# A Restormer block on one core: an order written by a list scheduler, the tensor-engine convolution in 5 of 8 bands, two taps added by DMA, LayerNorm statistics in batches

## The chip, the core and the metric

One Trainium2 chip; the kernel runs on one of its cores, and the others are idle. The metric is device time in microseconds (us). Engines are named as in the profile: PE (TensorE, matmuls), DVE (VectorE), ACT (ScalarE), POOL (GpSimd) and SP (SyncE, which here only issues DMAs).

## The reference

One transformer block on 16 images of 128 channels and 96 x 96 pixels, all in float32. Cut to what matters:

```python
xn1 = layernorm(x_hwc, ln1_w, ln1_b)                 # over the 128 channels of each pixel
q, k, v = xn1 @ wq.T, xn1 @ wk.T, xn1 @ wv.T         # 8 heads of 16 channels
attn = softmax(einsum('bhcn,bhdn->bhcd', l2norm(q), l2norm(k)) * 16 ** -0.5)   # 16 x 16 per head
x = x + (einsum('bhcd,bhdn->bhcn', attn, v) merged over heads) @ wp.T
xn2 = layernorm(x_hwc, ln2_w, ln2_b)
h1 = einsum('bchw,oc->bohw', xn2, w_in)              # 128 -> 512 channels
h2 = depthwise 3 x 3 convolution of h1, padding 1    # 512 channels
x = x + einsum('bchw,oc->bohw', gelu(h2), w_out)     # 512 -> 128 channels
```

The attention is over channels, so for one image it is a 128 x 128 matrix that is applied to every pixel.

## The kernel before

An image is cut into 24 **units** of 4 rows (384 pixels, three tiles of 128) and 8 **bands** of 12 rows (three units). Channels lie on the partitions. An image goes through these steps:

- **LN1** (`ln1_unit`, with `normalised`), once per unit: PE transposes three 128 x 128 tiles to PSUM (L175), DVE takes their statistics (`bn_stats` L179, `bn_aggr` L180) and adds eps (`ve`, L182), POOL raises the variances to the power -0.5 (`rstd`, L184), DVE makes the shift (`nb`, L186), ACT applies scale and shift (L189), PE transposes back (L195) and adds the tile's products to the Gram matrix (L206), and ACT copies the normalised pixels into one of two padded image buffers `xn` (L210).
- **The matrix** (`attention`): some 30 small dependent operations make one 128 x 128 matrix for the image from its Gram matrix.
- **LN2** (`ln2_unit`), once per unit: PE multiplies the matrix with the unit (L298), DVE adds result and x (L300), and then the LayerNorm steps follow as above, with L302 at the end.
- **FFN**, once per band and each of four chunks of 128 hidden channels. Three chunks go `by_taps`: PE makes the hidden rows (L311, three matmuls), ACT copies them to SBUF (L314) and makes the first tap into the accumulator tile `h3` (L315), DVE adds the other eight taps one by one to `h3` in place (L318), and ACT applies Gelu (L321). This is called a **job** below. The fourth chunk goes `by_matmuls`: `w_in` and the convolution as one 3 x 3 convolution, nine matmuls a unit into PSUM (L330), with Gelu on ACT (L334).
- **Output** (`ffn_out`), once per unit: four matmuls (L340), DVE adds x (L345), and a band is stored by a DMA from SP.

The order of the work is that of the loops at the end: while the FFN of image i runs band by band, the list `beside` holds LN1 of image i + 1, the matrix, and LN2 two bands ahead, and its entries are dealt out between the steps of the band. The framework's own scheduler may move instructions a little within an engine's queue. Each engine executes its queue in order. x is loaded once and stays in SBUF from LN1 until the band is stored (`xpool`, 13 bands).

Of the kernel before, what the change touches and what calls it, by code (L numbers as in the profile page):

```python
# [22 lines left out]
def tile_restormer_block(  # L23
# [134 lines left out]
    h1p = ctx.enter_context(tc.tile_pool(name="h1p", bufs=2))  # L158
    h3p = ctx.enter_context(tc.tile_pool(name="h3p", bufs=2 * NCH))
# [7 lines left out]
    def x_unit(i, u):  # L167
        b, s = divmod(u, UPB)
        return xbs[i, b][:, s * UT : (s + 1) * UT]

    def normalised(xt, name):
        """z of a unit, with the pixels on the partitions (SBUF) and back on the free axis (PSUM)."""
        pT = p_tr.tile([P, TPU, P], F32, tag="tr", name=f"pT_{name}")
        for j in range(TPU):
            nc.tensor.transpose(pT[:, j, :], xt[:, j * P : (j + 1) * P], ident)  # L175
        st = small.tile([P, TPU, 6], F32, tag="st", name=f"st_{name}")
        mv = small.tile([P, TPU, 2], F32, tag="mv", name=f"mv_{name}")
        for j in range(TPU):
            nc.vector.bn_stats(st[:, j, :], pT[:, j, :])  # L179
            nc.vector.bn_aggr(mv[:, j, :], st[:, j, :])  # L180
        ve = small.tile([P, TPU], F32, tag="ve", name=f"ve_{name}")
        nc.vector.tensor_scalar(ve, mv[:, :, 1], EPS, None, ALU.add)  # L182
        rstd = small.tile([P, TPU], F32, tag="rstd", name=f"rstd_{name}")
        nc.gpsimd.tensor_tensor(rstd, ve, mhalf[:, :TPU], ALU.pow)  # L184
        nb = small.tile([P, TPU], F32, tag="nb", name=f"nb_{name}")
        nc.vector.scalar_tensor_tensor(nb, mv[:, :, 0], -1.0, rstd, ALU.mult, ALU.mult)  # L186
        zT = xhp.tile([P, TPU, P], F32, tag="zT", name=f"zT_{name}")
        for j in range(TPU):
            nc.scalar.activation(  # L189
                zT[:, j, :], pT[:, j, :], AF.Identity,  # L190
                bias=nb[:, j : j + 1], scale=rstd[:, j : j + 1],
            )
        pB = p_tr.tile([P, UT], F32, tag="tr", name=f"pB_{name}")
        for j in range(TPU):
            nc.tensor.transpose(pB[:, j * P : (j + 1) * P], zT[:, j, :], ident)  # L195
        return zT, pB

    grams, sums, mats = {}, {}, {}

    def ln1_unit(i, u):  # L200
        if u == 0:
            grams[i] = p_g.tile([P, P], F32, tag="g", name=f"g_{i}")
            sums[i] = keep.tile([P, NU], F32, tag="sums", name=f"sums_{i}")
        zT, pB = normalised(x_unit(i, u), f"a{i}_{u}")
        for j in range(TPU):
            nc.tensor.matmul(  # L206
                grams[i], lhsT=zT[:, j, :], rhs=zT[:, j, :],
# [221 lines left out]
```

## Time and profile before

| | |
|---|---|
| timed runs | 6691.94, 6692.86, 6698.94 us; median 6692.86 |
| profiled execution | its time is its span, 6694.6 us from the first to the last instruction |
| PE busy | 5776.3 us, 86% |
| DVE busy | 5447.8 us, 81% |
| ACT busy | 3065.7 us, 46% |
| POOL busy | 1158.9 us, 17% |
| DMA traffic | 155.62 MB, mean 23 GB/s |

Busy time is the union of an engine's instructions, DMA issues left out. A matmul's end is modelled, and successive matmuls overlap, so PE's busy time holds more than the array's work. A float32 matmul appears as two rows (x3456 matmuls of the composite convolution as x6912). In the chain of work each piece begins where the one before it released it, so the pieces of one engine in a row are the steps from one start to the next, shorter than the instruction's own record.

### The profile page before, as it was taken

The page shows a single profiled execution, that of the slowest core. Times are in us where ns is not written, and L with a number is a line of the kernel's source. Part 1 is how long each engine was busy: PE and PEld are TensorE (multiplying, and loading weights), DVE is VectorE, ACT ScalarE, POOL GpSimd, SP SyncE. Part 2 cuts the span into 40 slices and gives each one's busy share as a digit, 9 for nine tenths or more (in the row PEclk, how much of TensorE's full clock was granted, in tenths as well). Part 3 has the DMA queues.
Part 4 walks back from the last instruction along what each step waited for, and adds up shares of the span by engine and source line. Part 5 has one row for each costly group of instructions (what it writes and reads, how often), then busy time and mean ns, then how long its engine had stood idle before and what let it go on. Part 6 is the DMA issues. An engine that isn't in the chain of part 4 may idle for free.

```text
span 6694.6 us, 59531 instructions
## 1 busy us (share of the span) xinstructions
PE 5776.3 (86%) x20421; PEld 3234.1 (48%) x20421; DVE 5447.8 (81%) x10303; ACT 3065.7 (46%) x5808; POOL 1158.9 (17%) x802
## 2 busy tenths in 40 slices
PE   4888889888888888888888898888988889888899
PEld 3444445444454454544444454444544445444454
DVE  2778878888888888888888888887888888888899
ACT  2444444444444444444444444444444444444443
POOL 1111211212112111111212112121121211211100
PEclk6899999999999999999999999999999999999999
DMA  1000000000000000000000000000000000000000
GB/s 51 15 22 15 29 22 22 22 29 22 22 26 25 22 22 22 29 22 22 25 25 22 29 22 22 22 22 29 22 22 22 29 22 22 22 29 22 11 15 22
DMA packets 39520, 155.62 MB, mean 23 GB/s; under 512 B 5296, under 2 KB 6320, under 8 KB 39216
## 3 DMA queue, kind: packets, MB, share of 16 engines
q1 hardware_dynamic: 36864, 151.01, 6.6%
q8 instruction: 160, 2.62, 0.2%
q14 instruction: 144, 1.18, 0.1%
q10 hardware_dynamic: 2352, 0.81, 0.0%
HBM read 76.30 MB, written 75.50 MB: 23 GB/s over the span
## 4 chain that ended last, share of the span: by engine, by line
DVE 52%; PE 23%; POOL 16%; ACT 4%; issue 4%; POOLq 0%; DMA 0%; ACTq 0%
DVE h L318 37%; POOL rstd_a L184 10%; PE pc L330 7%; POOL rstd_b L184 6%; PE ph L311 4%; DVE st_a L179 3%; DVE st_b L179 3%; PE pB_b L195 3%; DVE xb L300 2%; PE g L206 2%; PE po L340 2%; PE pT_b L175 2%; ACT zT_b L189 1%; DVE mv_a L180 1%; PE pB_a L195 1%
## 5 line engine op out<-in xcount | busy, mean ns | idle before, releaser
L318 DVE SCALAR_TENSOR_TENSOR h<-h,dw,h 128x1152 f32<-128x1152 f32 x3072 | 4293.9, 1407 | 15.5 <-ACT h L315 7.9
L330 PE MATMUL pc<-xn,comp 128*128 128x384 f32 x6912 | 2386.4, 491 | 0.0
L330 PEld LDWEIGHTS pc<-xn,comp 128*128 128x128 f32 x6912 | 1281.4, 192 | 881.1 <-ACT h L314 80.8
L340 PE MATMUL po<-h,woutT 128*128 128x384 f32 x3072 | 1154.2, 502 | 187.9 <-ACT h L321 109.0
L184 POOL TENSOR_TENSOR rstd_a<-ve_a,mhalf 128x3 f32<-128x3 f32 x384 | 688.7, 1793 | 2835.2 <-DVE ve_a L182 2441.1
L311 PE MATMUL ph<-xn,winT 128*128 128x490 f32 (+1 forms) x2304 | 1040.3, 569 | 47.3 <-ACT h L314 40.7
L189 ACT ACTIVATE zT_a<-pT_a,nb_a,rstd_a 128x128 f32<-128x128 f32 x1152 | 443.4, 454 | 988.8 <-DVE nb_a L186 988.8
L340 PEld LDWEIGHTS po<-h,woutT 128*128 128x128 f32 x3072 | 555.3, 192 | 648.0 <-ACT h L321 171.8
L184 POOL TENSOR_TENSOR rstd_b<-ve_b,mhalf 128x3 f32<-128x3 f32 x384 | 439.8, 1145 | 2390.0 <-DVE ve_b L182 2086.4
L314 ACT COPY h<-ph 128x490 f32<-128x490 f32 (+1 forms) x1152 | 610.8, 541 | 386.1 <-PE ph L311 383.9
L321 ACT ACTIVATE h<-h 128x1152 f32<-128x1152 f32 x384 | 446.8, 1164 | 677.3 <-DVE h L318 677.3
L195 PE MATMUL pB_a<-ident,zT_a 128*128 128x128 f32 x1152 | 357.6, 314 | 344.8 <-ACT zT_a L189 343.9
L189 ACT ACTIVATE zT_b<-pT_b,nb_b,rstd_b 128x128 f32<-128x128 f32 x1152 | 442.8, 453 | 449.8 <-DVE nb_b L186 449.6
L311 PEld LDWEIGHTS ph<-xn,winT 128*128 128x128 f32 x2304 | 391.5, 194 | 482.8 <-ACT h L314 149.3
L179 DVE BATCH_NORM_STATS2 st_b<-pT_b 128x6 f32<-128x128 f32 x1152 | 296.9, 280 | 328.0 <-PE pT_b L175 327.5
L334 ACT ACTIVATE h<-pc 128x384 f32<-128x384 f32 x384 | 188.4, 491 | 807.9 <-PE pc L330 807.9
L315 ACT ACTIVATE h<-h,dw 128x1152 f32<-128x1152 f32 x384 | 483.2, 1258 | 9.1
L195 PE MATMUL pB_b<-ident,zT_b 128*128 128x128 f32 x1152 | 354.5, 316 | 131.3 <-ACT zT_b L189 118.2
L206 PE MATMUL g<-zT_a 128*128 128x128 f32 x2304 | 447.5, 293 | 0.0
L195 PEld LDWEIGHTS pB_a<-ident,zT_a 128*128 128x128 f32 x1152 | 170.7, 148 | 569.3 <-ACT zT_a L189 565.0
L206 PEld LDWEIGHTS g<-zT_a 128*128 128x128 f32 x2304 | 402.5, 219 | 3.1 <-issue 3.1
L195 PEld LDWEIGHTS pB_b<-ident,zT_b 128*128 128x128 f32 x1152 | 162.0, 141 | 458.0 <-ACT zT_b L189 402.4
(101 smaller groups left out, 3506.5 us busy)
## 6 DMA issues: line engine op xcount, KB each, us to landing
xb<-in_x_dram SPq DMA_DIRECT2D x128, 576.0 KB, 3.8
out_dram<-xb SPq DMA_DIRECT2D x128, 576.0 KB, 2.8
win_sb<-in_L_conv_w_in_dram ACTq DMA_DIRECT2D x1, 256.0 KB, 10.9
wout_sb<-in_L_conv_w_out_dram ACTq DMA_DIRECT2D x1, 256.0 KB, 12.5
wv_sb<-in_L_conv_wv_dram ACTq DMA_DIRECT2D x1, 64.0 KB, 4.7
wqk_sb<-in_L_conv_wq_dram ACTq DMA_DIRECT2D x1, 64.0 KB, 2.5
wqk_sb<-in_L_conv_wk_dram ACTq DMA_DIRECT2D x1, 64.0 KB, 2.4
wp_sb<-in_L_conv_wp_dram ACTq DMA_DIRECT2D x1, 64.0 KB, 4.1
```

The lines of the kernel that those rows point to most:

```text
L179: nc.vector.bn_stats(st[:, j, :], pT[:, j, :])
L184: nc.gpsimd.tensor_tensor(rstd, ve, mhalf[:, :TPU], ALU.pow)
L189: nc.scalar.activation(zT[:, j, :], pT[:, j, :], AF.Identity, bias=nb[:, j : j + 1], scale=rstd[:, j : j + 1],)
L195: nc.tensor.transpose(pB[:, j * P : (j + 1) * P], zT[:, j, :], ident)
L206: nc.tensor.matmul(grams[i], lhsT=zT[:, j, :], rhs=zT[:, j, :], start=(u == 0 and j == 0), stop=(u == NU - 1 and j == TPU - 1),)
L311: nc.tensor.matmul(ph, lhsT=winT[:, n, :], rhs=xn[:, r0 + r : r0 + r + k, :], start=True, stop=True)
L314: nc.scalar.copy(h1[:, r : r + k, :], ph)
L315: nc.scalar.activation(h3, h1[:, 0:BR, 0:W], AF.Copy, scale=dw[:, n, 0:1])
L318: nc.vector.scalar_tensor_tensor(h3, h1[:, dy : dy + BR, dx : dx + W], dw[:, n, t : t + 1], h3, ALU.mult, ALU.add)
L321: nc.scalar.activation(h3, h3, AF.Gelu)
L330: nc.tensor.matmul(pc, lhsT=comp[:, t, :], rhs=xn[:, r : r + UR, dx : dx + W], start=(t == 0), stop=(t == 8),)
L340: nc.tensor.matmul(rows(po), lhsT=woutT[:, n, :], rhs=hs[n][:, s * UR : (s + 1) * UR, :], start=(k == 0), stop=(k == NCH - 1),)
```

## The change

The loops at the end are replaced by a planner in the source. Every operation is entered in a list with its engine, a supposed duration, a place (a number that says how urgent it is), and what it reads and writes; `Plan.order` then plays engines and buffers through with these supposed durations, takes on each free engine the ready operation with the lowest place, and the operations are emitted in the order of their supposed starts, under `tc.manual_schedule()`, so that the framework moves none. The supposed time until an adding DMA has landed is `T_ADD`, 6500 ns. With it:

- The composite convolution on PE is used only in bands 1, 3, 5, 6 and 7; in bands 0, 2 and 4 the fourth chunk goes by taps too. Its nine matmuls a unit are nine entries of the list.
- Of a job's taps, ACT makes taps 1 and 2 as products in tiles `pr`; POOL issues a DMA that adds the second product to the first, and, after DVE's six other taps, one that adds the sum to `h3`. Gelu follows that DMA.
- LayerNorm works on batches of two units: the six tiles' `bn_stats` are combined by five DVE operations instead of `bn_aggr` and `ve`, and power and `nb` are made once per batch.
- x is loaded twice: for LN1 into a pool of two bands, and again for LN2 into one of six bands.
- PSUM: transposes back have a buffer of their own, outputs one instead of two, and the matrix step works in the Gram matrix's bank.

```diff
-UR = 4  # image rows of a unit: 384 tokens, three tiles of 128
...
+PE_BANDS = (1, 3, 5, 6, 7)
+DMA_TAPS = (1, 2)
+BU = 2
+ATT = 3.0
+LEAD = 3.0
+X1_BUFS, XB_BUFS, H1_BUFS, PR_BUFS, H3_BUFS = 2, 6, 3, 3, 9
+IN_TURN = ("h3", "h1", "pr", "xb", "x1")
+IN_ORDER = ("PE", "DVE", "ACT")
+SLACK = 300
+T_ADD = 6500
...
+        def dispatch(engine, time):
+            queue = queues[engine]
+            while queue:
+                item = heapq.heappop(queue)
+                k = item[1]
+                lacks = room(k)
+                if lacks is None:
+                    break
+                waiting.setdefault(lacks, []).append(k)
+            else:
+                return
...
+        return [ops[k][3] for k in sorted(range(len(ops)), key=lambda k: (starts[k], k))]
...
-    xpool = ctx.enter_context(tc.tile_pool(name="xpool", bufs=NB + 5))
+    xpool = ctx.enter_context(tc.tile_pool(name="xpool", bufs=XB_BUFS))
+    x1pool = ctx.enter_context(tc.tile_pool(name="x1pool", bufs=X1_BUFS))
     p_tr = ctx.enter_context(tc.tile_pool(name="p_tr", bufs=3, space=PSUM))
+    p_b = ctx.enter_context(tc.tile_pool(name="p_b", bufs=1, space=PSUM))
     p_h = ctx.enter_context(tc.tile_pool(name="p_h", bufs=2, space=PSUM))
-    p_o = ctx.enter_context(tc.tile_pool(name="p_o", bufs=2, space=PSUM))
+    p_o = ctx.enter_context(tc.tile_pool(name="p_o", bufs=1, space=PSUM))
...
+        def moments():
...
+            nc.vector.tensor_tensor(dm, st[:, :, 1], st[:, :, 4], ALU.subtract)
+            nc.vector.scalar_tensor_tensor(q, st[:, :, 2], C * EPS, st[:, :, 5], ALU.add, ALU.add)
+            nc.vector.tensor_tensor(m2, st[:, :, 1], st[:, :, 4], ALU.add)
+            nc.vector.scalar_tensor_tensor(dm, dm, 0.25, dm, ALU.mult, ALU.mult)
+            nc.vector.scalar_tensor_tensor(ve, q, 1.0 / C, dm, ALU.mult, ALU.add)
...
+        def by_dma(to, of):
+            nc.gpsimd.dma_start(out=to, in_=of, accum_op=ALU.add)
...
+        act(t_act(BR * W), j - 0.6, first_tap, h1, h3)
+        for k, t in enumerate(DMA_TAPS):
+            act(t_act(BR * W), j - 0.4 + 0.5 * k, lambda t=t: product(t), h1, [("pr", (jn, t))])
+        pr = [("pr", (jn, t)) for t in DMA_TAPS]
+        for k, t in enumerate(DMA_TAPS[1:]):
+            op("POOL", 900, j + 0.5, lambda t=t: by_dma(d["pr", DMA_TAPS[0]], d["pr", t]), [pr[1 + k]], [pr[0]], T_ADD)
+        left = [t for t in range(1, 9) if t not in DMA_TAPS]
+        for k, t in enumerate(left):
+            dve(t_dve(BR * W), j + k / len(left), lambda t=t: tap(t), h1, h3)
+        if pr:
+            op("POOL", 900, j + 1, lambda: by_dma(h3s[g, n], d["pr", DMA_TAPS[0]]), [pr[0]], h3, T_ADD)
+        act(t_act(BR * W), j + 1.5, lambda: nc.scalar.activation(h3s[g, n], h3s[g, n], AF.Gelu), [], h3)
...
+    with tc.manual_schedule():
+        for work in plan.order():
+            work()
```

The order that results differs at every place. Three of them follow.

DVE, in the middle of the program, before (`mv`, `ve` and `nb` are LayerNorm's small tiles, `h3_7_3_0` the accumulator of image 7, band 3, chunk 0):

```order
L318 SCALAR_TENSOR_TENSOR h3_7_3_0_19333<-h1_7_3_0_19337,dw_98,h3_7_3_0_19333 128x1152
L182 TENSOR_SCALAR ve_b7_14_19309<-mv_b7_14_19302 128x3
L318 SCALAR_TENSOR_TENSOR h3_7_3_0_19333<-h1_7_3_0_19337,dw_98,h3_7_3_0_19333 128x1152
L186 SCALAR_TENSOR_TENSOR nb_b7_14_19313<-mv_b7_14_19302,rstd_b7_14_19311 128x3
L318 SCALAR_TENSOR_TENSOR h3_7_3_0_19333<-h1_7_3_0_19337,dw_98,h3_7_3_0_19333 128x1152 x2
```

and DVE in the change, at the start of image 7 (`h3_56_1` is the accumulator of the 57th band, chunk 1; `xTrue` is x as loaded for LN2; `dm`, `q`, `m2` are the batch's small tiles):

```order
L389 TENSOR_TENSOR dm_b7_3_17577<-st_b7_3_17553 128x6
L390 SCALAR_TENSOR_TENSOR q_b7_3_17578<-st_b7_3_17553 128x6
L391 TENSOR_TENSOR m2_b7_3_17576<-st_b7_3_17553 128x6
L392 SCALAR_TENSOR_TENSOR dm_b7_3_17577<-dm_b7_3_17577 128x6
L393 SCALAR_TENSOR_TENSOR ve_b7_3_17579<-q_b7_3_17578,dm_b7_3_17577 128x6
L623 SCALAR_TENSOR_TENSOR h3_56_1_17503<-h1_56_1_17475,dw_104,h3_56_1_17503 128x1152
L691 TENSOR_TENSOR xTrue_6_7_16117<-po_55_0_17533,xTrue_6_7_16117 128x384
L623 SCALAR_TENSOR_TENSOR h3_56_1_17503<-h1_56_1_17475,dw_104,h3_56_1_17503 128x1152
L401 SCALAR_TENSOR_TENSOR nb_b7_3_17602<-m2_b7_3_17576,rstd_b7_3_17588 128x6
L623 SCALAR_TENSOR_TENSOR h3_56_2_17574<-h1_56_2_17536,dw_104,h3_56_2_17574 128x1152 x3
```

One tap stood between `ve` and `nb`; now two taps and an add do. Taps on one tile follow each other more often.

POOL before, around the matrix step of an image (its power is `rn`), with what an instruction waits for:

```order
L184 TENSOR_TENSOR rstd_b_22_15359<-ve_b_22_15357,mhalf 128x3 [waits DVE_49,Activation_49,Pool_49]
L184 TENSOR_TENSOR rstd_b_23_15395<-ve_b_23_15393,mhalf 128x3 [waits DVE_49,Activation_49,Pool_49]
L257 TENSOR_TENSOR rn_15467<-n_6_15465,mhalf 128x2 [waits DVE_49]
L184 TENSOR_TENSOR rstd_b_0_15550<-ve_b_0_15548,mhalf 128x3 [waits DVE_49,Activation_49,Pool_49]
L184 TENSOR_TENSOR rstd_b_1_15611<-ve_b_1_15609,mhalf 128x3 [waits DVE_49,Activation_49,Pool_49]
```

and in the change, in bands 53 and 54 (DMASW is the semaphore of an earlier adding DMA):

```order
L626 DMA h_53_1_16801<-pr_1_1_16843 128x1152 [waits DMASW2_49,DVE_49,PE_49]
L397 TENSOR_TENSOR rstd_a_0_16932<-ve_a_0_16916,mhalf 128x6 [waits DVE_49,Pool_49]
L626 DMA pr_2_1_16954<-pr_2_2_16959 128x1152 [waits DMASW4_49,DMASW1_49,Activation_49]
L397 TENSOR_TENSOR rstd_b_11_17033<-ve_b_11_17022,mhalf 128x6 [waits DVE_49,Pool_49]
L626 DMA h_53_2_16946<-pr_2_1_16954 128x1152 [waits DMASW4_49,DVE_49,PE_49]
L626 DMA pr_0_1_17029<-pr_0_2_17036 128x1152 [waits DMASW3_49,Activation_49]
L626 DMA h_54_0_17016<-pr_0_1_17029 128x1152 [waits DMASW6_49,DVE_49,PE_49]
```

The powers had the queue to themselves; now a power stands behind an addition to `h`, which waits for the job's first addition and for DVE's last tap.

ACT before, in band 5 of image 7 (`xn1` is an image buffer, `zT` normalised pixels, `pc` the composite convolution's result):

```order
L302 ACTIVATE xn1_223<-pB_b7_19_19939,b2_94,w2_92 128x4x96 [waits PE_49]
L334 ACTIVATE h3_7_5_3_19990<-pc_7_5_0_20041 128x384 [waits PE_49]
L189 ACTIVATE zT_b7_20_19971<-pT_b7_20_19953,nb_b7_20_19969,rstd_b7_20_19967 128x128 [waits DVE_49]
L189 ACTIVATE zT_b7_20_19971<-pT_b7_20_19953,nb_b7_20_19969,rstd_b7_20_19967 128x128 x2
L314 COPY h1_7_5_1_20082<-ph_7_5_1_0_20083 128x490 [waits PE_49]
```

and in the change, in bands 41 and 42:

```order
L436 ACTIVATE xn0_215,sums_6_12855<-pB_a6_4_8_13434 128x4x96 [waits PE_49]
L646 ACTIVATE h3_41_2_13251<-h3_41_2_13251 128x1152 [waits DMASW3_49]
L436 ACTIVATE xn0_215,sums_6_12855<-pB_a6_4_9_13450 128x4x96 [waits PE_49]
L606 COPY h1_42_1_13415<-ph_42_1_10_13457 128x392 [waits PE_49]
L615 ACTIVATE h3_42_1_13463<-h1_42_1_13415,dw_104 128x1152 [waits Activation_49]
L668 ACTIVATE h3_41_3_13220<-pc_41_2_13378 128x384 [waits PE_49]
L615 ACTIVATE pr_42_1_1_13475<-h1_42_1_13415,dw_104 128x1152
L615 ACTIVATE pr_42_1_2_13488<-h1_42_1_13415,dw_104 128x1152 [waits DMASW4_49]
```

A Gelu (L646) now waits for an adding DMA, and LayerNorm's last step, copies and products stand behind it.

## Rows read from the trace of the kernel before

**Rows 1.** The page, part 1: busy us, share of the span, instructions.
```profile
span 6694.6 us, 59531 instructions
...
PE 5776.3 (86%) x20421; PEld 3234.1 (48%) x20421; DVE 5447.8 (81%) x10303; ACT 3065.7 (46%) x5808; POOL 1158.9 (17%) x802
```

**Rows 2.** Windows: stretch, length, busy us by engine (x instructions), clock, DMA share, GB/s.
```profile
0.00:210.00 210.00, 104.20 (x397) 76.24 (x397) 55.38 (x296) 55.07 (x147) 28.87 (x49) 0.68 0.12 41
210.00:6694.00 6484.00, 5672.08 (x20024) 3157.82 (x20024) 5392.40 (x10008) 3010.68 (x5662) 1130.03 (x753) 0.97 0.07 23
1011.00:1062.00 51.00, 47.94 (x162) 26.98 (x163) 49.48 (x77) 23.56 (x41) 6.76 (x5) 1.00 0.07 24
```

**Rows 3.** Waits of DVE: who waited for whom, us in total, times, longest.
```profile
DVE st_b L179 <- PE pT_b L175: 327.5, 243, 3.9
DVE nb_b L186 <- POOL rstd_b L184: 309.2, 357, 1.4
DVE nb_a L186 <- POOL rstd_a L184: 275.1, 362, 1.1
```

**Rows 4.** Chain of work, 3100 to 3135 us: start, us, what.
```profile
3101.57 0.09 DVE mv_a L180
...
3101.84 1.32 DVE h L318
...
3107.48 0.08 DVE ve_a L182
...
3110.21 0.07 DVE nb_a L186
```

**Rows 5.** Chain of work, the last 60 us.
```profile
6632.51 5.81 PE pc L330 x18
...
6640.89 2.42 PE ph L311 x6
...
6680.75 0.02 issue
6680.77 1.43 DVE h L318
```

**Rows 6.** The page, part 5: groups of ACT (busy us, mean ns | idle before).
```profile
L314 ACT COPY h<-ph 128x490 f32<-128x490 f32 (+1 forms) x1152 | 610.8, 541 | 386.1 <-PE ph L311 383.9
L321 ACT ACTIVATE h<-h 128x1152 f32<-128x1152 f32 x384 | 446.8, 1164 | 677.3 <-DVE h L318 677.3
...
L334 ACT ACTIVATE h<-pc 128x384 f32<-128x384 f32 x384 | 188.4, 491 | 807.9 <-PE pc L330 807.9
L315 ACT ACTIVATE h<-h,dw 128x1152 f32<-128x1152 f32 x384 | 483.2, 1258 | 9.1
```

**Rows 7.** Timeline of POOL: the first and last power of image 0, one beside taps.
```profile
30.30 0.86 POOL L184 TENSOR_TENSOR rstd_a<-ve_a,mhalf 128x3 f32<-128x3 f32 x1 [0.59 <-DVE ve_a L182]
...
161.87 0.85 POOL L184 TENSOR_TENSOR rstd_a<-ve_a,mhalf 128x3 f32<-128x3 f32 x1 [4.42 <-DVE ve_a L182]
...
3107.73 1.86 POOL L184 TENSOR_TENSOR rstd_a<-ve_a,mhalf 128x3 f32<-128x3 f32 x1 [11.33 <-ACT h L334]
```

**Rows 8.** The page, parts 3 and 6: load and store queue; issues, KB, us to landing.
```profile
q1 hardware_dynamic: 36864, 151.01, 6.6%
...
xb<-in_x_dram SPq DMA_DIRECT2D x128, 576.0 KB, 3.8
out_dram<-xb SPq DMA_DIRECT2D x128, 576.0 KB, 2.8
...
wout_sb<-in_L_conv_w_out_dram ACTq DMA_DIRECT2D x1, 256.0 KB, 12.5
```

**Rows 9.** Timeline of the SP queue: one issue.
```profile
3017.92 0.34 SPq L347 DMA_DIRECT2D out_dram<-xb  x1
```

More of the change, by code (lines that the diff above doesn't have):

```diff
@@ L165, in rows, with x_unit @@
         return t.rearrange("p (r w) -> p r w", w=W)
-    def x_unit(i, u):
+    def x_unit(of, i, u):
         b, s = divmod(u, UPB)
[L169 to L191, printed above, removed]
-            )
[L193 to L207, printed above, removed]
-                start=(u == 0 and j == 0), stop=(u == NU - 1 and j == TPU - 1),
-            )
-        nc.scalar.activation(
-            interior(i, u), rows(pB), AF.Identity, accum_out=sums[i][:, u : u + 1]
-        )
@@ L295, in ln2_unit @@
[L295 to L304 removed]
+        return of[i, b][:, s * UT : (s + 1) * UT]
@@ new lines, in pe, with dve, act, load @@
+    def pe(ns, p, f, r, w):
+        op("PE", ns, p, f, r, w, ns + 200 + SLACK)
+    def dve(ns, p, f, r, w):
+        op("DVE", ns, p, f, r, w, ns + 130 + SLACK)
+    def act(ns, p, f, r, w):
+        op("ACT", ns, p, f, r, w, ns + 250 + SLACK)
+    def load(p, i, b, second):
+        def go():
+            pool, of = (xpool, xbs) if second else (x1pool, x1s)
+            t = pool.tile([P, BR * W], F32, tag="x", name=f"x{second}_{i}_{b}")
+            nc.sync.dma_start(out=t, in_=xv[i, :, b * BR * W : (b + 1) * BR * W])
+            of[i, b] = t
+        key = "xb" if second else "x1"
+        op("SP", 100, p, go, [], [(key, (i, b), s) for s in range(UPB)], 6000)
@@ L402, in tile_restormer_block, with add, store @@
-    for step in outs:
-        step()
+        def add():
+            xt = x_unit(xbs, i, s + b * UPB)
+            nc.vector.tensor_add(xt, d["po"], xt)
+        def store():
+            nc.sync.dma_start(out=ov[i, :, b * BR * W : (b + 1) * BR * W], in_=xbs[i, b])
+        for k, n in enumerate(order):
+            pe(t_mm(UT), p + 0.05 * k, lambda k=k, n=n: product(k, n), [("h3", (g, n), s)], [po])
+        dve(t_dve(UT), p + 0.2, add, [po], [("xb", (i, b), s)])
+        if s == UPB - 1:
+            op("SP", 100, p + 0.3, store, [("xb", (i, b), k) for k in range(UPB)], [], 6000)
@@ new lines, in tile_restormer_block, with job_of @@
+    NG = B * NB
+    jobs, first = [], []
+    for g in range(NG):
+        first.append(len(jobs))
+        jobs += [(g, n) for n in range(NCH) if not (composite(g) and n == PE_CHUNK)]
+    first += [len(jobs) + 3 * k for k in range(3)]
+    def job_of(g):
+        if g < 0:
+            return 3.4 * g
+        lo = int(g)
+        return first[lo] + (g - lo) * (first[lo + 1] - first[lo])
+    NBT = NU // BU
+    for i in range(B):
+        begin2 = job_of(NB * i - 1) - LEAD
+        due1 = begin2 - ATT
+        begin1 = job_of(NB * (i - 1)) if i else due1 - 8
+        for k in range(NBT):
+            s = begin1 + (due1 - begin1) * k / NBT
+            for u in range(k * BU, (k + 1) * BU):
+                if u % UPB == 0:
+                    load(s - 2, i, u // UPB, False)
+            norm_batch(s, i, k, False)
+        attention(due1, i)
+        for k in range(NBT):
+            s = job_of(NB * i + (BU * k - UPB) / UPB) - LEAD
+            for u in range(k * BU, (k + 1) * BU):
+                if u % UPB == 0:
+                    load(s - 2, i, u // UPB, True)
+            norm_batch(s, i, k, True)
+        for g in range(NB * i, NB * (i + 1)):
+            for j in range(first[g], first[g + 1]):
+                conv_job(j, *jobs[j])
+            start, end = first[g], first[g + 1]
+            for s in range(UPB):
+                if composite(g):
+                    by_matmuls(start + 1 + s * (end - start) / UPB, g, s)
+                ffn_out(end + 1.5 + 0.8 * s, g, s)
```

530 lines of the change are left out of this document (367 added, 163 removed).

## The prediction

> **What bounds the kernel now.** I read the shares of the page first: over a span of 6694.6 us PE is busy 86%, DVE 81%, ACT 46% [rows 1]. The three timed runs have a median of 6692.9, 1.7 us under that span, so the sum below is made against the span and nothing is added for what lies around it. Two engines near 85% and no full one says: two nearly equal loads that wait for each other. The windows tell where [rows 2]. The first 210 us hold the LayerNorm of image 0 alone, with DVE busy 55.4; from there DVE is busy 5392.4 of 6484, or 83.2%, and leaves 1092 us idle. In the best stretch I found it reaches 49.48 of 51, or 97.0%, so the engine can be filled. The waits say what opens the gaps [rows 3]: the statistics wait for PE's transposes (327.5 for LN2 alone), and `nb` waits 309.2 and 275.1 for POOL's power. None of it is missing data from HBM: the load and store queue holds the 16 DMA engines for 6.6% of the span [rows 8].
>
> So there are two levers: less work on DVE and PE, and fewer gaps. The change pulls both.
>
> **DVE, part by part**, in steps from the start of one operation to the next as the chain shows them [rows 4].
> Taps: 27 jobs an image with six taps in place of 24 with eight: 2592 for 3072, 480 fewer x 1.32 us = -634.
> Same-tile taps: the last four taps of the kernel all write one tile, and there a step is 1.43 + 0.02 of issue = 1.45 [rows 5], 0.13 more than behind another operation. Counted in the two orders, 206 taps now directly follow a tap on the same tile, and 1113 will (the first place above ends with a run of three): 907 x 0.13 = +118.
> Aggregation leaves: 2304 x 0.09 = -207. `ve` and `nb` of single units leave: 768 x (0.08 + 0.07) = -115.
> Batches add five small operations and one `nb`, 384 times. No row shows the five. All at 0.08 (the `ve` row) is the lower end, 0.47 for the six; all five at twice that, because each waits for a result, is the upper, 0.87. Two of the five read what was just written, so I take 3 x 0.08 + 2 x 0.16 + 0.07 = 0.63, +242 (ends +180 and +334).
> The 2304 statistics, residuals, adds and the matrix step stay.
> Sum: -634 + 118 - 207 - 115 + 242 = -596; DVE's busy time goes from 5447.8 to about 4852 (ends 4790 and 4944).
>
> **PE.** The composite conv leaves three of eight bands: 144 units x 9 = 1296 products. A unit's nine take 5.81 us [rows 5], so -836. In its place come 48 jobs' first convolutions of 2.42 each, +116. The page's busy goes from 5776.3 to about 5056. Much of that count is ends of matmuls that nothing overlaps while PE waits, so I hold DVE for the fuller engine; the other reading is a rival below.
>
> **ACT** gets the two products of each job: 1296 first and extra taps for 384, 912 x 1.258 = +1147; copies 144 x 0.541 = +78; 48 large Gelus x 1.164 = +56, and 144 small ones fewer, -71 [rows 6]. From 3065.7 to about 4276.
>
> **DMA and POOL.** 128 more loads and 864 adding transfers. A plain 576 KB transfer holds the 16 engines 0.066 x 6694.6 / 256 = 1.73 us [rows 8]. An adding one must read two tiles and write one: from 1.73 (if only the writing counts) to four times that, 6.9; I take twice, 3.46. Then 864 x 3.46 + 384 x 1.73 = 3654 us of the span: hidden, at 72%. The loads of LN2's own copy of x are issued at least 1.7 jobs (some 19 us) ahead of their use in the steady part of the order; with that cover gone a load would cost its 3.8. On POOL the powers halve to 384 x 1.86 = 714 [rows 7], and an issue costs between SP's 0.34 [rows 9] and a whole power's 1.86: 294 to 1607. Either way POOL is under half full; what counts is what stands behind what. The second place above shows a power behind an addition that waits for the last tap of a job; such a wait holds LayerNorm back, not DVE, as long as other jobs' taps stand ahead on DVE. They do: between `ve` and `nb` the new order puts over 2.8 us of other DVE work in 330 of 384 batches, against at most one tap in nearly all of the 768 units now. That removes most of the 584 us of `nb` waits.
> How long an addition takes to land is not shown. Stores land after 2.8, loads after 3.8, a weight load at the start after 12.5 [rows 8]. I take a load and a store in a row, 3.8 + 2.8 = 6.6, practically the 6.5 that the source's table supposes. Two follow each other in a job. The first runs beside the job's own six taps (8 us); the second ends in front of a Gelu, and ACT executes in order: copies, products and normalisations of later units stand behind that Gelu (third place). So any landing over 6.5 stops ACT.
>
> **The sum.** Conv part: (4852 - 55) / 0.97 = 4945. I take the 97.0% of the best stretch because the new order cuts PE's products into single entries between which transposes go, covers `nb`, and makes DVE alone the fullest engine; 83.2% is the other end. First part: now the powers run from 30.30 to 161.87 in steps of 5.7 [rows 7]; 12 batches of two units, each such a step and the second unit's scaling and placing (3 x 0.36 and some 0.6), would take at most 12 x 7.4 = 89, and overlap; I take 75 for 137, so 150 for 210. Tail: one landing more behind the last tap, +8. Together 4945 + 150 + 8 = **5103**, taken as 5100. Ends of the small operations and of the first part move this by -80 to +110.
>
> In the conv part ACT is then busy 4276 - 55 = 4221 of 4945, which leaves 724 / 432 = 1.68 us a job for waiting.
>
> **A rule weighed.** POOL's power takes 0.85 with DVE idle and 1.86 beside a tap [rows 7], 1.0 more. If an issue suffers the same once, the addition lands after 7.6, 1.1 beyond the supposed 6.5, inside ACT's 1.68: the sum stays. The Trainium skill speaks against the change here: "SBUF — State Buffer", section "SBUF: two separate sides", says that descriptors of a DMA issued on POOL starve while DVE runs an operation that holds the port they share, and has 620 ns grow to 3100. As an estimate from the Trainium skill's figures, 2.5 us more would land at 9.1 and cost (9.1 - 6.5 - 1.68) x 432 = 400, a time of 5500; no run here shows such a DMA. The same mechanism, priced from rows, is the first rival.
>
> **Rivals.**
> *Late additions stop ACT* (chance 0.20). If the issue is held by two taps (2 x 1.41), an addition lands after 9.4, and each job waits 9.4 - 6.5 - 1.68 = 1.2 us beyond its slack: 432 x 1.2 = 520, so 5620. For it: POOL's rows beside taps, and the order that leaves no operation to spare. Against it: slack also lies on DVE and PE, and taps that run slower than the source's table thinks give the additions time.
> *PE is the bound.* If its 5056 are all work: (5056 - 104) / 0.97 + 158 = 5263. This is inside my forecast's own range and shares its chance.
> *No better filled than now* (0.07): 4797 / 0.832 + 158 = 5924. For it: ACT goes from 46% to over 80%, a third engine that can hold the other two; PSUM for the outputs drops from two buffers to one. Against it: the waits of rows 3 are the ones that the new order covers.
> *The DMA engines become the bound* (0.10), the one that ends slower. If adding runs at a quarter of a copy's rate, 864 x 6.9 + 664 = 6626, with the first part 6776. It decides from 6.8 us an addition on, where 864 x 6.8 + 664 + 150 reaches the time before; from 5.0 on it costs anything. For it: nothing in this trace adds in a DMA, and the volume goes from 256 transfers to over 1200. Against it: two reads and a write are work for two, not four.
> That the change does not do what it says is excluded by the order, which holds 864 additions, 2160 composite products and 384 powers.
>
> **How the numbers follow.** Forecast 5100 with its own range 4950 to 5350: 0.58. Late additions, 5350 to 6100: 0.20. Fill as now: 0.07. DMA bound, slower: 0.10. Faster than 4950 (fill over 99% or cheap small operations): 0.04. About no change: 0.01. A difference of 0.2% (13 us) is about what a measurement of this kernel can tell. Faster: 0.88, within: 0.02, slower: 0.10. The range 4930 to 5950 leaves out the slower cases, the uppermost late ones and a little below.
>
> **What would show it.** Right: DVE's taps x2592 near 1.4 us each and DVE at 94% or more from about 150 us on; `nb` hardly waiting for POOL; ACT's Gelu (L646) waiting little for a DMA; additions landing after 5 to 8 us; DMA share near 70%. Wrong: a long ACT wait in front of L646, with landings of 9 us or more; DMA share at 95%; DVE at 83% with its waits on PE; or statistics and small operations of the batches at twice the price I gave.

## The result, and the profile after

The changed kernel takes **5210.6 us** (median of 4 runs, 5205.5 to 5215.5) beside 6692.4 for the kernel before on the same chip: a ratio of 0.7782 [0.7771, 0.7793]. The prediction was 5100, range 4930 to 5950. The profiled execution has a span of 5205.4 us.

The page, part 1 (busy us, share of the span, instructions), which answers to [rows 1]:

```profile
span 5205.4 us, 55115 instructions
...
PE 4771.6 (92%) x18118; PEld 2835.9 (54%) x18118; DVE 4736.2 (91%) x8288; ACT 4002.6 (77%) x6768; POOL 1592.3 (31%) x1282
```

The two fullest engines have lost busy time (PE 1005 us, DVE 712), ACT has gained 937, and the two are now above 90% where they stood at 86 and 81. The windows are the counterpart of [rows 2]: the first part, the rest, and four bands of one image in the middle (3 with the composite convolution, 4 with four tap jobs, 6 and 7 with the composite).

```profile
0.00:150.00 150.00, 99.06 (x478) 76.41 (x478) 57.42 (x282) 59.51 (x172) 27.24 (x37) 0.82 0.25 77
150.00:5205.00 5055.00, 4672.51 (x17640) 2759.54 (x17640) 4678.77 (x8006) 3943.13 (x6597) 1565.07 (x1245) 0.98 0.66 144
...
1848.60:1880.90 32.30, 29.09 (x124) 17.76 (x123) 31.91 (x52) 28.20 (x51) 11.55 (x9) 1.00 0.72 152
1880.90:1930.90 50.00, 44.78 (x177) 26.02 (x176) 45.44 (x90) 40.04 (x73) 19.14 (x13) 1.00 0.63 140
1969.00:2004.80 35.80, 35.80 (x127) 21.05 (x126) 32.08 (x47) 26.27 (x40) 10.00 (x8) 1.00 0.62 133
2004.80:2039.80 35.00, 35.00 (x117) 20.23 (x116) 31.69 (x46) 23.74 (x35) 9.96 (x8) 1.00 0.63 136
```

Of the 5055 us from 150 on, DVE is busy 4678.77, or **92.6%**, and PE 4672.51, or 92.4%. The bands show what that mean is made of: in band 3 DVE is full (31.91 of 32.30) and PE has gaps, in bands 6 and 7 PE is full (35.80 of 35.80, 35.00 of 35.00) and DVE has gaps, and in band 4 neither is.

DVE's waits (us in total, times, longest), beside [rows 3]:

```profile
DVE xTrue L691 <- PE po L684: 131.8, 83, 7.8
DVE h L623 <- ACT h L615: 90.5, 76, 2.6
DVE st_a L380 <- PE pT_a L374: 59.2, 34, 3.7
DVE st_b L380 <- PE pT_b L374: 39.0, 37, 2.8
...
DVE nb_a L401 <- POOL rstd_a L397: 7.8, 14, 0.9
```

The wait of `nb` for POOL's power has gone from 584 us to under 9 (7.8 here, LN2's 0.9), that of LN2's statistics from 327.5 to 39.0. What leads now is the last add of an output unit, which waits for PE's sum.

Groups of the page's part 5 (busy us, mean ns of one | idle just before, what ended most of it); ACT's answer to [rows 6]:

```profile
L623 DVE SCALAR_TENSOR_TENSOR h<-h,dw,h 128x1152 f32<-128x1152 f32 x2592 | 3649.8, 1414 | 130.9 <-ACT h L615 90.5
...
L606 ACT COPY h<-ph 128x490 f32<-128x490 f32 x1296 | 697.8, 546 | 466.2 <-PE ph L599 456.1
L626 POOL DMA_DIRECT2D h<-pr x432 | 396.0, 917 | 1687.1 <-DVE h L623 455.6
...
L646 ACT ACTIVATE h<-h 128x1152 f32<-128x1152 f32 x432 | 507.1, 1174 | 255.1 <-DMA h<-pr 254.2
L397 POOL TENSOR_TENSOR rstd_b<-ve_b,mhalf 128x6 f32<-128x6 f32 x192 | 426.4, 2221 | 727.7 <-DVE ve_b L393 708.3
L626 POOL DMA_DIRECT2D pr<-pr x432 | 412.3, 954 | 655.8 <-ACT pr L615 604.1
```

ACT's Gelu (L646) waits 254.2 us for the adding transfers; ACT's larger wait is for PE's first convolution (456.1). Parts 3 and 6 (queue, packets, MB, share of 16 engines; issues, KB, us to landing), beside [rows 8]:

```profile
q0 software_dynamic: 124416, 509.66, 52.2%
q1 hardware_dynamic: 55296, 226.52, 12.5%
...
pr<-pr POOLq DMA_DIRECT2D x432, 576.0 KB, 6.1
h<-pr POOLq DMA_DIRECT2D x432, 576.0 KB, 5.0
xFalse<-in_x_dram SPq DMA_DIRECT2D x128, 576.0 KB, 4.7
xTrue<-in_x_dram SPq DMA_DIRECT2D x128, 576.0 KB, 4.8
out_dram<-xTrue SPq DMA_DIRECT2D x128, 576.0 KB, 5.0
```

An adding transfer holds the 16 engines 0.522 x 5205.4 / 864 = **3.14 us** and lands after 6.1 (the first of a job) and 5.0 (the second). Loads and stores land later than the 3.8 and 2.8 of before.

DVE's steps in band 3, from the chain of waits (start, us, what), are the counterpart of [rows 4]:

```profile
1856.94 0.17 DVE dm_a L389
1857.11 0.08 DVE q_a L390
1857.18 0.08 DVE m_a L391
1857.26 0.09 DVE dm_a L392
1857.35 0.02 issue
1857.37 0.17 DVE ve_a L393
1857.54 1.34 DVE h L623
1858.88 0.03 issue
1858.90 1.43 DVE h L623
...
1861.77 0.08 DVE nb_a L401
```

Here no engine but DVE is on the chain. The six operations of this batch cost 0.17 + 0.08 + 0.08 + 0.09 + 0.17 + 0.08 = 0.67 with 0.02 of issue between, a tap 1.34, and one right behind a tap on the same tile 1.43 with 0.02 to 0.03 of issue.

### The profile page after: what moved, and what is told of

The parts are those of the page before. It is cut to its first block, busy times and chain, and to the rows that moved or that the text cites. A ratio compares the mean times of both kernels' runs of the same rounds, so it can differ in the third digit from the quotient of the medians.

```text
span 5205.4 us, 55115 instructions
## 1 busy us (share of the span) xinstructions
PE 4771.6 (92%) x18118; PEld 2835.9 (54%) x18118; DVE 4736.2 (91%) x8288; ACT 4002.6 (77%) x6768; POOL 1592.3 (31%) x1282
## 4 chain that ended last, share of the span: by engine, by line
DVE 46%; PE 35%; ACT 8%; DMA 7%; issue 3%; POOL 2%; POOLq 0%; ACTq 0%
DVE h L623 33%; PE pc L660 15%; PE ph L599 7%; PE po L684 7%; DMA h<-pr 4%; DVE st_a L380 3%; DVE st_b L380 2%; ACT pr L615 2%; DMA pr<-pr 2%; DVE xTrue L368 2%; DVE xTrue L691 2%; PE pm L364 2%; PE g L424 2%; ACT h L615 1%; ACT zT_a L408 1%
## 5 line engine op out<-in xcount | busy, mean ns | idle before, releaser
L623 DVE SCALAR_TENSOR_TENSOR h<-h,dw,h 128x1152 f32<-128x1152 f32 x2592 | 3649.8, 1414 | 130.9 <-ACT h L615 90.5
L660 PE MATMUL pc<-xn,comp 128*128 128x384 f32 x4320 | 1580.8, 492 | 43.3 <-ACT h L606 23.4
L599 PE MATMUL ph<-xn,winT 128*128 128x490 f32 (+1 forms) x2592 | 1226.7, 566 | 136.8 <-ACT h L606 117.2
L660 PEld LDWEIGHTS pc<-xn,comp 128*128 128x128 f32 x4320 | 800.3, 192 | 622.5 <-issue 159.2
L615 ACT ACTIVATE pr<-h,dw 128x1152 f32<-128x1152 f32 x864 | 1067.4, 1258 | 68.4 <-DMA pr<-pr 67.3
L606 ACT COPY h<-ph 128x490 f32<-128x490 f32 x1296 | 697.8, 546 | 466.2 <-PE ph L599 456.1
L626 POOL DMA_DIRECT2D h<-pr x432 | 396.0, 917 | 1687.1 <-DVE h L623 455.6
L646 ACT ACTIVATE h<-h 128x1152 f32<-128x1152 f32 x432 | 507.1, 1174 | 255.1 <-DMA h<-pr 254.2
L397 POOL TENSOR_TENSOR rstd_b<-ve_b,mhalf 128x6 f32<-128x6 f32 x192 | 426.4, 2221 | 727.7 <-DVE ve_b L393 708.3
L626 POOL DMA_DIRECT2D pr<-pr x432 | 412.3, 954 | 655.8 <-ACT pr L615 604.1
L397 POOL TENSOR_TENSOR rstd_a<-ve_a,mhalf 128x6 f32<-128x6 f32 x192 | 383.0, 1995 | 493.3 <-DVE ve_a L393 486.1
L364 PE MATMUL pm<-xn,mwT 128*128 128x384 f32 x768 | 320.7, 501 | 3.6 <-ACT h L606 3.5
```

What stands on the lines that cost most here:

```text
L397: nc.gpsimd.tensor_tensor(rstd, d["ve"], mhalf[:, :n], ALU.pow)
L599: nc.tensor.matmul(ph, lhsT=winT[:, n, :], rhs=xn[:, r0 + r : r0 + r + k, :], start=True, stop=True)
L606: nc.scalar.copy(d["h1"][:, r : r + min(5, BR + 2 - r), :], d.pop(("ph", r)))
L615: nc.scalar.activation(to, window(t), AF.Copy, scale=dw[:, n, t : t + 1])
L623: nc.vector.scalar_tensor_tensor(h3, window(t), dw[:, n, t : t + 1], h3, ALU.mult, ALU.add)
L626: nc.gpsimd.dma_start(out=to, in_=of, accum_op=ALU.add)
```

## The experiments

The kernel before ran beside these twelve at 6694.1 to 6698.7 us; the brackets are 95% intervals of the ratio to it. An edit is shown against the changed kernel. Two questions stood at the start. Does the gain come from work taken off DVE and PE (the division), or from gaps closed by the order? And of the time that is left, is DVE the bound, or PE, or ACT with its adding transfers?

**1. The order without the new division.** All eight bands composite, no adding transfers: the old amount of work in the new order, with batches.

```
-PE_BANDS = (1, 3, 5, 6, 7)
-DMA_TAPS = (1, 2)
+PE_BANDS = (0, 1, 2, 3, 4, 5, 6, 7)
+DMA_TAPS = ()
```

> The list order and the batches alone: the composite convolution in all 8 bands and no taps by DMA, as the kernel before shares its work out. By steps measured in the changed kernel DVE has 480 taps more (x 1.37 = 658, busy about 5390) and PE 1296 products more and 48 first convolutions less (+721, busy about 5490). Theory A (the order fills the two engines, the smaller work does the rest): filled as in the changed kernel, PE 5490 x 1.091 = 5990, so 5850 to 6050. Rival B (the order brings little, the work that was taken away brought the gain): near the fill of the kernel before, 6500 or more.

Measured: **5576.2 us**, ratio 0.8326 [0.8314, 0.8339]. Its windows (same columns as above):

```profile
0.00:150.00 150.00, 99.70 (x482) 76.82 (x483) 57.39 (x282) 59.92 (x174) 27.19 (x37) 0.86 0.25 77
150.00:5573.00 5423.00, 5273.34 (x19942) 3146.49 (x19940) 5318.19 (x8486) 2897.75 (x5636) 810.04 (x381) 1.00 0.13 40
```

DVE is busy 5318.19 of 5423, 98.1%, PE 97.2%. Order, buffers and batches without any new division take off 1119 us of the 1485 from the 6695.3 beside it; the new division adds 366. It is a larger share than either theory gave it. The division without the order was not run, so 366 is its worth behind the order. TensorE's clock is in the 1119 too: of its two levels, 2.4 and 1.2 GHz, it stands at the lower one for 513 us of the kernel before (mean 0.962 of full speed) and for 51 us of run 1 (0.996). A composite product takes 0.645 us at the higher and 1.28 at the lower, so that is worth at most half the difference, 231 us, of PE's time.

**2 and 3. The two halves of the division, one at a time.** First the five bands without adding transfers, then the transfers with eight composite bands.

```
-DMA_TAPS = (1, 2)
+DMA_TAPS = ()
```

> The changed kernel with all eight taps on DVE and no adding DMA; the composite convolution stays in 5 bands. DVE has 864 taps more (x 1.37 = 1184, busy about 5920), PE as in the change. Theory A: DVE alone is the bound and can be filled to 97 or 98%, so 6050 to 6150. Rival C (additions that land late are what keeps the changed kernel from its sum): DVE's fill would rise well over that of the change by the absence of additions alone, and ACT waits for no DMA; the time would be the same 6050, but then the run with later planned landings gains as well.

```
-PE_BANDS = (1, 3, 5, 6, 7)
+PE_BANDS = (0, 1, 2, 3, 4, 5, 6, 7)
```

> Two taps by DMA as in the change, but the composite convolution in all 8 bands as before: PE +721 (busy about 5490), DVE 288 taps fewer (busy about 4340). Theory A: PE alone is the bound and full, 5490 / 0.98 + 100 = 5700, so 5600 to 5750; the 5 bands are worth some 500 us. Rival D (PE has room, its busy time is mostly ends of matmuls): 5200 or less, since DVE has less to do.

Measured: 2 takes **6374.0** (0.952 [0.9505, 0.9534]), 3 takes **5318.3** (0.7942 [0.7929, 0.7955]). Without the transfers the 48 added jobs put 384 taps back on DVE, which is busy 5921.9 us (93%): 798 us slower than the old division ordered by the same planner, and a miss of the 6050 to 6150 that both readings had. With eight composite bands PE is full, as theory A had it, but at 5248.6 us busy and not 5490:

```profile
150.00:5316.00 5166.00, 5150.85 (x19945) 3170.81 (x19943) 4334.29 (x7719) 3724.81 (x6405) 1336.17 (x1150) 1.00 0.59 130
```

So five bands pay only because DVE was relieved first, and then bring 108 us more, much less than I expected of them: eight bands leave PE at 5150.85 of 5166, and five leave no engine that full.

**4. Statistics by the unit.**

```
-BU = 2
+BU = 1
```

> Batches of one unit in place of two, so 384 times more the six small DVE operations and the power. DVE +384 x 0.6 = 230. Theory A (DVE is the bound in about two thirds of the time, PE in the rest): +120 to +200, so 5330 to 5410. Rival (the batch is worth more by the waits it saves, since the power of POOL stands behind the additions): 5500 or more.

Measured: **5198.6**, 0.7763 [0.7751, 0.7774], that is 12 us less, the same within what a measurement tells, and not 120 to 200 slower. DVE is busy 157 us more (4892.8) and fills its time to 94%; the power of image 0's matrices comes at 87.5 us in place of 117.2, so the first part is 30 us shorter. Batches of two take work off DVE that does not turn into time here. Nor is it they that close the power's waits, which are small here too (DVE's waits of run 4):

```profile
DVE nb_b L401 <- POOL rstd_b L397: 16.4, 21, 1.0
DVE nb_a L401 <- POOL rstd_a L397: 8.9, 10, 1.0
```

**5, 6, 9 and 12. Four cuts in one and the same order:** the last product of each composite unit (PE), the last of DVE's six taps, both at once, and ACT's second product with the transfer that adds it.

```
         def product(t):
+            if t == 8:
+                return
...
-                start=(t == 0), stop=(t == 8),
+                start=(t == 0), stop=(t == 7),
```

> Same order, but the ninth product of every composite unit is left out (the convolution lacks its last tap there): PE -240 x 9 of nothing else, that is 240 products x 0.646 = -155 us; nothing changes on DVE, ACT, POOL or the DMAs. Theory A (PE is the full engine in bands 5, 6 and 7, where 9 of an image's 15 composite units lie, DVE elsewhere): 144 x 0.646 = -93, and up to -155, so 5055 to 5120. Rival C (late additions and ACT hold the others): 5190 to 5215.

```
         def tap(t):
+            if t == 8:
+                return
```

> Same order, but the last of DVE's six taps of every job is left out (the convolution lacks it): 432 x 1.37 = -592 us on DVE and nothing else. If DVE were the bound all along, -550, so 4650. Theory A: PE's 4772 then bounds more and more of the time, 4772 / 0.98 + 100 = 4970, so 4900 to 5020. Rival C: additions no earlier for ACT, so 5100 or more.

Run 9 has both edits.

> Both cuts of the two runs before at once, in the same order of instructions: the ninth product of each composite unit and the last of VectorE's six taps of every job are left out (so part of the convolution is missing). TensorE some 4630 us busy, VectorE some 4180, ScalarE and the transfers as in the changed kernel. Theory A (two engines take turns as the bound, band by band, so each covers the other's removed work): the two cuts together are worth clearly more than the 12 + 126 = 138 us that they were worth apart; 4930 to 5030 us. Theory B (the ring of ScalarE product, adding transfers and gelu, with the waits in its queues, sets the band once VectorE is out of the way): no more than the cut on VectorE alone, 5060 to 5090 us, with ScalarE's waits for a transfer as large as before or larger. Plain sum: about 5070 us, which would not tell A from B by the time alone; then the waits decide.

```
         def product(t, to=None):
+            if t == DMA_TAPS[1]:
+                return
...
-op("POOL", 900, j + 0.5, lambda t=t: by_dma(...), ...)
+op("POOL", 900, j + 0.5, lambda: None, ...)
```

> The third of the cuts in the order of the changed kernel: the second product of every job and the transfer that adds it to the first are left out (so one of the nine taps is missing). ScalarE loses 432 x 1.25 = 540 us of its 4003, the transfers 432 of 864; the instructions of TensorE and VectorE stay as they are, in their order. Theory A (TensorE and VectorE take turns as the bound and ScalarE and the transfers only follow): VectorE's and TensorE's waits for ScalarE shrink a little, 5130 to 5200 us. Theory B (the ring of ScalarE product, two adding transfers and gelu sets the band in many places): more than the cut on VectorE gave, below 5080 us. Loads and stores should land faster again: loads 3.8 to 4.3 us instead of 4.7, and VectorE's taps keep their 1.41 us if the transfers do not slow them.

| cut | busy time of the profile | time | against 5210.6 | interval of the ratio to before |
|---|---|---|---|---|
| PE (5) | PE 4772 to 4696 | 5198.9 | -12 | 0.7751 to 0.7777 |
| DVE (6) | DVE 4736 to 4178 | 5084.2 | -126 | 0.7583 to 0.7606 |
| PE and DVE (9) | PE 4648, DVE 4177 | 5045.2 | -165 | 0.752 to 0.7542 |
| ACT and transfers (12) | ACT 4003 to 3528, transfers 864 to 432 | 5170.9 | -40 | 0.7715 to 0.774 |

No cut is worth what it takes off its engine: 558 us of DVE give 126, and the 12 of PE's cut are within what a measurement tells. "VectorE is the bound" and "TensorE is the bound" fall, and the turn-taking theory too in the form that run 9 priced: the two cuts together give 165, little more than their sum of 138, not 180 to 280. Run 5 lies in the range of rival C, run 6 between theory A and rival C, run 12 in the range of theory A. Run 9 lies between its two theories, and the waits that were to decide do not bear out B as it was put: ACT's Gelu waits 212.8 us for an addition, less than the 254.2 of the changed kernel. ACT's work and the first additions are no bound by themselves: with half the transfers the time moves 40. But the second addition stays in run 12, and Gelu still waits for it:

```profile
L648 ACT ACTIVATE h<-h 128x1152 f32<-128x1152 f32 x432 | 504.1, 1167 | 270.4 <-DMA h<-pr 269.2
```

In run 9 nothing is full, as its page says:

```profile
PE 4648.5 (92%) x17638; PEld 2761.3 (55%) x17638; DVE 4177.4 (83%) x7856; ACT 3990.7 (79%) x6768; POOL 1581.3 (31%) x1282
```

Part 4 of the pages tells more: the chain of work that ended last, in shares of the span by engine, for the changed kernel and runs 6, 9 and 12.

```profile
DVE 46%; PE 35%; ACT 8%; DMA 7%; issue 3%; POOL 2%; POOLq 0%; ACTq 0%
...
PE 54%; DVE 14%; DMA 13%; ACT 12%; POOL 3%; issue 3%; POOLq 0%; ACTq 0%
...
PE 39%; ACT 20%; DVE 15%; DMA 15%; issue 5%; POOL 5%; POOLq 0%; ACTq 0%
...
DVE 56%; PE 39%; ACT 2%; issue 2%; DMA 1%; POOL 0%; ACTq 0%; POOLq 0%
```

Each cut moves the chain onto what was not cut: DVE's onto PE, ACT and the transfers; both together onto ACT and the transfers (35%); run 12's back onto DVE and PE. So three things seem to take turns, DVE, PE, and the ring of ACT's products, additions and Gelus, and a cut of one or two is covered by the rest. This is read from the chains afterwards; no run cuts all three. Bands 5 to 7 of an image, from their first tap on DVE to the next image's, show the same: 107.8 us in the changed kernel (mean of 14 images), 106.8 with PE's cut, 107.9 with DVE's, 106.1 with both, 106.9 in run 12. DVE's gain lies in bands 0 to 4, 210.4 to 202.6.

The order of each queue stays the same in these runs; in run 12 a job takes one tile of `pr` in place of two. Run 12 also shows what the transfers do to others; its loads and stores, beside the 4.7, 4.8 and 5.0 above:

```profile
h<-pr POOLq DMA_DIRECT2D x432, 576.0 KB, 4.9
xFalse<-in_x_dram SPq DMA_DIRECT2D x128, 576.0 KB, 3.9
xTrue<-in_x_dram SPq DMA_DIRECT2D x128, 576.0 KB, 3.8
out_dram<-xTrue SPq DMA_DIRECT2D x128, 576.0 KB, 2.9
```

**7. A later planned landing.**

```
-T_ADD = 6500
+T_ADD = 9000
```

> The planner supposes 9.0 us until an addition has landed in place of 6.5, so it places the Gelus later behind them. Rival C (ACT's 254 us of waiting for additions in front of Gelu are on the path): 100 to 250 less, 4960 to 5110. Theory A (those waits are covered): 5180 to 5240.

Measured: **5335.1**, 0.797 [0.7958, 0.7982], 125 us slower. Its two groups:

```profile
L606 ACT COPY h<-ph 128x490 f32<-128x490 f32 x1296 | 699.7, 545 | 564.2 <-PE ph L599 552.0
...
L646 ACT ACTIVATE h<-h 128x1152 f32<-128x1152 f32 x432 | 502.8, 1164 | 11.5 <-DMA h<-pr 11.3
```

The Gelu no longer waits for a transfer (11.3 us for 254.2), and the time gets worse: an order made around a longer landing closes this wait and is a worse one. Whether the 254 us cost time in the changed kernel's own order is not shown by it, since the rest of the order differs too.

**8. Five bands, spread differently.**

```
-PE_BANDS = (1, 3, 5, 6, 7)
+PE_BANDS = (0, 2, 4, 5, 7)
```

> The composite convolution still in 5 of 8 bands, but in 0, 2, 4, 5 and 7 in place of 1, 3, 5, 6 and 7: three of them beside the next image's LN1, and no three in a row. The same work on every engine. Theory A (PE full and DVE at 87% in bands 5 to 7, DVE full elsewhere): the two even out, some 10 us an image, 100 to 250 less, 4960 to 5110. Rival (the places do not matter, waits of single operations do): 5180 to 5240.

Measured: **5444.1**, 0.8129 [0.8117, 0.8141]: 233 us slower with the same instructions. My expectation had the wrong sign. That this even spread of the composite bands fills both engines better under this planner is refuted; why the set is so much worse was not followed up.

**10 and 11. Two buffers for the output sums, and then another due time.** Both have statistics by the unit; run 11 differs from run 10 in `LEAD = 3.5` for 3.0 alone.

```
-BU = 2
+BU = 1
-p_tr = ctx.enter_context(tc.tile_pool(name="p_tr", bufs=3, space=PSUM))
+p_tr = ctx.enter_context(tc.tile_pool(name="p_tr", bufs=2, space=PSUM))
-p_o = ctx.enter_context(tc.tile_pool(name="p_o", bufs=1, space=PSUM))
+p_o = ctx.enter_context(tc.tile_pool(name="p_o", bufs=2, space=PSUM))
-tr=3, b=1, h=2, o=1, g=1, ...
+tr=2, b=1, h=2, o=2, g=1, ...
```

> Statistics by the unit, and one of the three PSUM buffers of the transposes given to the sums of the output (two instead of one). Theory A (too few buffers between the engines: VectorE's last add of a unit and TensorE's next sum wait for each other through the one buffer, 132 us of waits on VectorE and as many on TensorE): 5080 to 5160 us, with the wait of the add for the sum mostly gone. Theory B (the fill is set by the order as a whole, not by this buffer): within 30 us of the 5198.6 us of statistics by the unit, or slower where the transposes now wait for their second buffer.

> As the run with two output buffers, and the due time of the second normalisation 3.5 jobs ahead of its band instead of 3. No work changes, only the order. Theory A (the order is a lottery of some 1 to 2% around a fill of 92 to 94% of VectorE): within 80 us of the run with two output buffers, either way. Theory B (the order is no longer what limits): within 15 us of it. A version faster than 5150 us would beat both kernels clearly.

Measured: 10 takes **5291.4** (0.7898 [0.7885, 0.7912]), 93 us more than run 4; 11 takes **5157.3** (0.7698 [0.7687, 0.771]), the fastest of all that do the whole work, 1.0% under the changed kernel. In run 10 the exchange of buffers moves a wait and does not close it. The last add waits 43.1 us for its sum (87.1 in run 4), as theory A had it, but the statistics wait 88.5 for the transposes (5.8 in run 4), which theory B allowed for:

```profile
DVE st_a L380 <- PE pT_a L374: 88.5, 61, 3.8
DVE xTrue L691 <- PE po L684: 43.1, 34, 7.2
```

Moving one due time by half a job is worth 134 us, more than the 80 that I allowed. The window of run 11:

```profile
150.00:5155.00 5005.00, 4629.53 (x17660) 2722.64 (x17659) 4844.05 (x10225) 3959.71 (x6603) 1962.26 (x1614) 0.99 0.67 146
```

DVE does 165 us more work there than in the changed kernel and is busy 96.8% of the stretch.

One rival to "the order" was not tested: the granted clock, which goes with most of these times. Its mean is 0.990 in run 11, 0.978 in the changed kernel, 0.976 in run 10, 0.975 in run 4, 0.958 in run 8 and 0.951 in run 7; as time at the lower level, 107, 228, 256, 257, 454 and 526 us. PE can lose at most half of that: against the changed kernel up to 113 of the 233 us of run 8 and all of the 125 of run 7, and up to 75 of the 134 between runs 10 and 11. It is not the clock alone, since run 10 has the clock of run 4 and is 93 us slower. Whether a low clock makes an order slow, or PE's waits in a slow order go with a low clock, no run separates.

## Why the prediction was right, and which step was off

**The forecast stands** (5100 for 5210.6, 2% low), in part by luck: two misses of the sum offset each other, as the last point of this list shows. The steps can be held against the trace one by one.

- *DVE's work, 4852 predicted, 4736 measured: 116 too much, in three places.* If each operation is counted to the start of the next, or to its own end where DVE then waits, the taps changed by -578 us (predicted -634 + 118 = -516), the small operations of LayerNorm by -172 (predicted -80), the statistics by +44 and the adds by -6 (both predicted 0). The taps behind a tap on the same tile are there as counted, 206 before and 1113 after, at 1.45 us each against 1.32 and 1.33. But a tap followed by a wait counts with its whole record of 1.41, and of those (1.5 us and more to the next start) there were 529 before and 117 after; so the mean tap went from 1.345 to 1.371, which is +68 and not +118. The small operations that left had waits behind them too and counted 399 us, not 322; a batch's six cost 0.59 on the mean for the predicted 0.63. Run 1, with all 3072 taps, shows -72 us in all for the -80 of the small operations, but only as a sum of taps +75, small operations -175, statistics +41 and adds -13.
- *PE, 5056 predicted, 4772 measured.* The view that much of PE's count was overhanging ends agrees with run 1: eight composite bands, as before, and 5373.0 us for 5776.3. Part of that is the clock, granted at 1.00 there from 150 us on for 0.97 before [rows 2]: at most 231 of the 403 us, by the times at the lower level given with run 1.
- *ACT, 4276 predicted, 4003 measured.* The groups add up as predicted (the large Gelus +60 for +56, the copies +87 for +78), but the records of neighbouring operations overlap where the engine runs without gaps: all of ACT's records sum to 4625 us, for 4003 busy, and before to 3357 for 3066.
- *Transfers.* 3.14 us of the 16 engines for 3.46; landings 6.1 and 5.0 for 6.6; share 66% for 72%; POOL 31% for under half, an issue at 0.92 to 0.95. The rival in which they become the bound would have needed 6.8 us.
- *Late additions.* The rival had them land after 9.4; they land after 6.1 and 5.0. The waits of Gelu for them (254.2 us) do not go with the time: 11.3 in run 7, which is slower, 107.9 in run 11, the fastest order, 269.2 in run 12. The Trainium skill's rule, "SBUF — State Buffer", section "SBUF: two separate sides", weighed there, does not show in this kernel: DVE is busy 92.6% of the time, the issue takes 0.92 to 0.95 us, and by the rule's estimate of 9.1 the time would have been 5500. The Trainium skill ties the rule there to DVE operations in a 2-port perf mode, with a float32 `tensor_copy` as its example, and that section does not name `scalar_tensor_tensor`. So it did not have to speak against the change, and these taps are no test of it.
- *First part, 150 predicted.* The power of image 0's matrices comes at 117.2 us where it came at 173.7; 56 of the 60 us that I counted.
- *The fill (DVE's busy share from 150 us on): the step that was mis-sized.* I took 97.0%; it is 92.6%, under the 94% that I named as a sign of being right. With the measured work of DVE, 4679 / 0.97 would be 4824 where the trace has 5055: +231. The overcounted work hid half of it: (4797 - 4679) / 0.97 = 122. What is left, 109, is the miss of the sum. The reason that I gave, that DVE alone would be the fullest engine, does not hold: PE is as full (92.4%), is the full one in bands 6 and 7, and has 35% of the chain, where DVE has 46%. The rival in which PE is the bound gave 5263, nearer than the 5103; but PE's cut is worth 12 us, so it is not borne out either.

What the fill hangs on was shown only in part. No cut of one engine's work opens it (runs 5, 6, 9, 12), and neither does a longer planned landing (7) or the exchange of a transposes' buffer for one of the outputs (10). Runs 8, 10 and 11, in which the instructions stay nearly the same and their order changes, move the time by +233, +93 and -41 us against the nearest kernel without their edit (the changed kernel, run 4, run 4). And 97% can be had: by the old division in the new order (98.1%), and by run 11 (96.8%). So the order, a list schedule's answer to guessed durations, decides the last five per cent, the clock that comes with it included; which waits in it cost them stays open.

Of the two levers that the prediction named, the gaps were the greater: 1119 of 1485 us came with the order, its buffers and its batches, 366 with the division behind them. In the changed kernel the batches are worth nothing measurable (run 4); what the order, the buffers and the second load of x are worth one by one was not run. The 584 us of waits for the power went, as the prediction said; without batches, with twice as many powers, 25 us of them are left (run 4), which agrees with its reason, other work on DVE between `ve` and `nb`.

## What to carry to other kernels

Where two engines stand near 85% and wait for each other, reorder before moving work: the order, with its buffers, took both above 96% here (run 1). With four resources two thirds full or more, cutting an engine's work in a fixed order bought a quarter of it or less; then try several orders of nearly the same work (due times, planned latencies) on the chip, since here the slowest was 5.6% above the fastest. After a cut, read which engines the chain of work has moved to, before calling one of them the bound. Predict such a kernel with the fill of a whole loop, not of its best 50 us. Take an engine's load from steps between starts, not from sums of records, and remember that a page's busy time holds the whole record where a wait follows.

## What the runs showed of the hardware that I had not expected

- Plain transfers land later beside adding ones, and DVE keeps its pace. Stores land after 2.8 us without them (run 1), 2.9 with 432 (run 12), 5.0 with 864; loads of `xTrue` after 3.7, 3.8 and 4.8. The tap takes 1413 or 1414 ns in all three. The number alone does not decide: run 10 has the same 864, and its stores land after 3.0, its loads of `xTrue` after 5.4.
- The first addition of a job lands later than the second, 6.1 against 5.0; with DVE at 82% (run 6) it is 5.5 and 5.0.
- A composite product takes 0.645 us from start to start where TensorE's clock stands at 2.4 GHz and 1.28 where it stands at 1.2 (medians of the kernel before and of the changed one).
- A power on 6 columns takes 1.32 to 1.35 us before the first tap and 2.0 to 2.2 on the mean of all; one on 3 columns takes 0.85 before the first tap [rows 7] and, in run 10, 1.57 to 1.58 on the mean. So halving the number of powers saves POOL less than half. DVE is not quite idle beside the two powers below; it takes statistics for about the first 0.5 us of each.

```profile
30.90 1.35 POOL L397 TENSOR_TENSOR rstd_a<-ve_a,mhalf 128x6 f32<-128x6 f32 x1 [1.36 <-DVE ve_a L393]
...
115.86 1.32 POOL L397 TENSOR_TENSOR rstd_a<-ve_a,mhalf 128x6 f32<-128x6 f32 x1 [5.40 <-DVE ve_a L393]
```
